# A gated delta-rule block with two WKV stages: a new order for the opening, gates' sums one slot later, and the first inverse in one piece

## The chip, the core and the metric

The kernel runs as one program on one core of a Trainium2 chip. The metric is device time in microseconds (us) of one execution; below, "the profiled execution" is one that was also traced. The engines are TensorE (PE, with its weight loads PEld), VectorE (DVE), ScalarE (ACT), GpSimd (POOL) and SyncE (SP, which issues DMAs).

## The reference

Everything is float32. The inputs are x and a side tensor of 4 batches x 512 tokens x 512 channels, a condition vector per batch, and weights. Cut to what matters:

```python
def wkv(r, k, w, u, cond):                     # v is k here
    tf = sigmoid(sum(cond)); decay = exp(-exp(w)) * (0.5 + 0.5 * tf)
    ek, ekv = exp(min(k, 30)), exp(min(k, 30)) * k
    nf, df = forward scans  a = a * decay + ekv  and  b = b * decay + ek
    nb, db = the same two scans backwards
    euk = exp(min(u + k, 30))
    num, den = nf + nb - ekv + euk * k, df + db - ek + euk
    return sigmoid(r) * num / max(den, 1e-8) * (0.8 + 0.2 * tf)

def attn(c):                                   # c = wkv(x, side, w1, u1, cond)
    q, k, v, z = c @ W_qkvz                    # 16 heads of q, k; 32 heads of v, z; 128 each
    b, a = c @ W_ba
    q, k, v = silu(causal convolution of 4 taps over tokens)
    beta, g = sigmoid(b), -exp(A_log) * softplus(a + dt_bias)
    q, k = rmsnorm(q), rmsnorm(k)              # and constant factors
    for each chunk, with g summed inside it:   # gated delta rule
        T = inverse of (1 + strictly lower part of beta * k k^T * exp(g_i - g_j))
        v_new = T (beta v) - T (beta k exp(g)) state
        out = q exp(g) state + (q k^T * decay) v_new;  state = decayed state + k^T v_new
    return (rmsnorm(out) * norm_w * silu(z)) @ W_out

x = x + attn(wkv(x, side, w1, u1, cond))
x = x + wkv(x, side, w2, u2, cond) @ binarized(ffn_w) + ffn_b
```

## The kernel before

**Units.** The work on the attention is cut into 64 units `n`: batch `b` and head pair `hq` (one head of q and k with its two heads of v and z), `divmod(n, 16)`. A unit works on all 512 tokens of its batch in four chunks of 128. Its weights come in six slabs `r`: q 0, k 1, v 2 and 3, z 4 and 5; in the first batch a slab is loaded raw (`wraw`), turned by PE (`ps_w`), copied by ACT (`w`) and stored for the later batches (`wsc`). Each of q, k and v goes through `project` (`ps_p`, four products), the first `tap` on ACT and three `taps` on DVE (`y`), then `silu`. `square` and `norms` give the norms; the reciprocal square root is a Newton iteration of 12 small operations (`root`, on POOL).

**The key side** of a unit runs six units ahead (`AHEAD`, `K`): `gap_load` brings the running sums of the gates from DRAM (`gsc`) to all partitions (`dkd`, and `dkt` for the query side), `gap_mask` (POOL) and `gap_exp` (ACT, 8 instructions) make decays of them, `key_pairs` (PE, `ps_kk`) and `key_matrix` (DVE, 8 instructions) the matrices, and `key_blocks` stores their 32 x 32 diagonal blocks (`blocks_m`). Four units are a group: their 128 blocks of 32 x 32 come back as one tile `L`, whose triangular inverses are made by 30 steps (`group_step`) of two instructions each. In the loop these run on POOL, for the first group on DVE. `group_end` stores them straight (`blocks_n`) and turned (`Lt`, `blocks_t`), and `inverse_load` brings a unit's own to the places where `inverse_1` to `inverse_4` (PE, with copies between) put the 128 x 128 inverse together: four loads of `inv_t` and six of `inv_n` for a unit, all on SP's queue.

**The gates** of a batch: `gates_product` (`ps_ba`, 32 products), `gates_exp` (ACT), `gates_series` (DVE, some 20 operations on 128 x 128), `gates_sum` (PE, `ps_g`), `gates_keep`, `gates_turn` (`ps_gt`), `gates_rows`, which stores `gsc`. Those of batch b+1 are made in the loop's iteration with `hq == 8`, three times in all.

**The order.** Each engine executes its instructions in the order in which the program writes them: the wrapper `InOrder` (line 80) keeps it, so every instruction of the profile stands under L80 and is told by its tile's name. The loop's iteration `i` walks `plan`, 22 slots of calls, each with an offset: `K` is unit i+6, `F` unit i (query, value, inverse), `C` unit i-1 (the chunks of the recurrence), `O` i-2 (output norm), `W` i-3 (output product). `("sub", m, n)` is a step of the next group, `("gate", f)` one of the gates, `("wkv", f)` a piece of the next batch's WKV, and `jobs` are calls added to a slot of one iteration.

**The opening** stands ahead of the loop. Loads of x and the side tensor go out on ACT's queue, constants on SP's. The first batch's WKV runs in four blocks of 128 channels with tiles lent from later work (`lent_...`): `first_mix` (POOL, a product), `first_scan` (DVE, two scans for "d" and two for "n"), `first_sum` (PE), `first_end` (DVE: limit, reciprocal, product; result `cT`). Its stages are put in an order by a shift of four stages a block, so that `first_mix` of the next block lies beside the scans of the one before. Then come the gates, the key sides of units 0 to 5 together, the first group's steps on DVE, and twenty `inverse_load` DMAs for units 0 and 1. Iteration 0 makes the query, value and z of unit 0, holds the matrices of units 4 and 5 till slot 13, and holds unit 0's inverse till slot 18:

```python
                    elif 0 <= i + rest[0] < NU:
                        if i == 0 and (f in INVERSE or f == gap_load and rest[0] > K):
                            later.append((f, *rest))
                        elif not (i == 0 and f == inverse_load or i == NU + 1 and f == out_start):
                            f(i + rest[0], *rest[1:])
```

PSUM's eight banks belong to tags with turns of their own ("pp" 2, "pj" 3, "inv" 1, "st" 2), and the four raw tiles of `ld` are shared by all slabs.

Of the kernel before, what the change touches and what calls it, by code (L numbers as in the profile page):

```python
# [40 lines left out]
def kernel(  # L41
# [104 lines left out]
    with ExitStack() as main:  # L146
# [24 lines left out]
        for cb in range(KT):  # L171
            at = slice(cb * P, (cb + 1) * P)
            raw = ld.tile([P, NC, P], F32, tag="raw", name=f"raw_k_first_{cb}")
            for t, src in ((raw, fside), (xs[0][:, :, at], x)):
                A.dma_start(out=t, in_=src[0, :, at].rearrange("(c p) d -> p c d", p=P))
            first_raw[cb] = raw

# [4 lines left out]
        for n, v in enumerate((w1, w2, u1, u2)):  # L182
            Q.dma_start(out=wu[:, n, :], in_=v.rearrange("(n p) -> p n", p=P))
        Q.dma_start(out=alog, in_=A_log.partition_broadcast(P))
# [17 lines left out]
        A.activation(nea, alog, AF.Exp)  # L202
        V.tensor_scalar_mul(nea, nea, -1.0)

# [128 lines left out]

        def gates_series(g, part):
# [13 lines left out]
            elif part == 2:  # L348
# [5 lines left out]
                V.tensor_scalar_add(beta[b], beta[b], 1.0)  # L354
                V.reciprocal(beta[b], beta[b])
# [8 lines left out]
        def gates_keep(g):  # L364
# [13 lines left out]
                gsum[b][:, 0].rearrange("p c (q r) -> p q c r", r=2),  # L378
            )

        def gates_turn(g):
            g["pt"] = bank("pj", f"ps_gt_{g['b']}")
            T.transpose(g["pt"][: NC * HV, :P], g["flat"][:, : NC * HV], ident)

        def gates_rows(g):
            b, n = g["b"], NC * HV
            rows = wkp.tile([P, S], F32, tag="d", name=f"sp_r_{b}")
            A.copy(rows[:n, :P], g["pt"][:n, :P])
# [143 lines left out]


# [36 lines left out]
        def key_root(n):  # L570
            root(*units[n]["kroot"])
            key_factors(n)
# [89 lines left out]
        def inverse_load(n):  # L662
# [3 lines left out]
            for d, at in enumerate(blocks):  # L666
# [3 lines left out]
                if d < 3:  # L670
                    for h in range(2):
                        Q.dma_start(
                            out=Tn[blocks[2 * h + (d > 0)], :, at],
                            in_=blocks_n[g, i, d, h * HM : (h + 1) * HM].rearrange("m i j -> i m j"),
                        )
# [363 lines left out]
        def last_add(b, c):  # L1039
# [33 lines left out]
             (slab_start, F, 3), ("gate", gates_series, 2), ("sub", 5, 25)],  # L1073

            [(project, F, 2, 0), (tap, K, 1, 0), (taps, K, 1), (head_end, O, 0),
             ("gate", gates_sum), ("wkv", wkv_mix), ("sub", 6, 26)],

            [(chunk_t, C, 1), (inverse_3, F), ("gate", gates_keep), (chunk_t_end, C, 1), (silu, K, 1),
             ("wkv", wkv_scan, "d", False), (slab_start, F, 0), ("sub", 7, 27)],

            [(project, F, 2, 1), (head_turn, O, 1), (slab_turn, F, 3), ("gate", gates_turn), (inverse_3_end, F), ("wkv", wkv_scan, "d", True),
# [396 lines left out]
```

## Time and profile before

| | |
|---|---|
| median of 3 runs | 3109.1 us (3107.02 to 3109.18) |
| profiled execution | 3108.79 us, its span 3107.0 us, mean granted PE clock 0.983 |
| busy | PE 2988.3 us (96%), DVE 2071.6 (67%), ACT 1866.0 (60%), POOL 1314.7 (42%) |
| instructions | 57961 |
| last block of the first WKV ends (`cT`, DVE) | 63.0 us from the span's start |
| last key matrix of group 0 ends | 114.2 |
| the closing copy `Lt` of the first group ends | 144.2 |
| iteration 1's first product (`ps_w<-vb,inv_t`) | 198.5 |
| iteration 2's first product | 242.4 |

The profile is of one execution. Busy shares are means over the whole span; a stretch of its own is read from the busy times by stretch, what an engine stood idle for from the waits ("engine and tile <- who released it: total, times, longest"), and the path that set the end from the chain of waits (start, duration, what). In all rows the time is in us from the span's start unless the text says otherwise. "Clock" is the share of TensorE's full clock that was granted.

### The profile page before, as it was taken

The numbers are of one execution on the slowest core, as the hardware profiler recorded it, in microseconds if no ns is written. First come the engines' busy times: TensorE is split into PE (matmuls) and PEld (weight loads), VectorE is DVE, ScalarE is ACT, GpSimd is POOL, SyncE is SP. The second block draws the span as 40 slices with busy tenths as digits, with TensorE's granted clock in tenths as the row PEclk, the third lists the DMA queues.
The fourth block names the chain that finished last, engine by engine and source line by source line (L and its number), as shares of the span: only waits on it lengthen the run. The fifth ranks groups of instructions, "written<-read, shape, count | busy, mean of one in ns | idle before, by whom it ended". The sixth has DMA issues, their size and how long they took to land.

```text
span 3107.0 us, 57961 instructions
## 1 busy us (share of the span) xinstructions
PE 2988.3 (96%) x20058; PEld 1978.5 (64%) x20058; DVE 2071.6 (67%) x4738; ACT 1866.0 (60%) x5119; POOL 1314.7 (42%) x3044
## 2 busy tenths in 40 slices
PE   6479999999999999999999999999999999999999
PEld 3346667666666666666666666666666666666665
DVE  7545776667655777777765787777766656577643
ACT  2446766667666666566666666566665666656552
POOL 3215445254432646355442636345451515255313
PEclk9689999999999999999999999999999999999999
DMA  3224544345343432323332332333332342323321
GB/s 75 90 82 139 145 121 131 111 130 156 110 139 101 129 93 82 109 81 114 104 94 76 118 104 82 88 101 115 94 97 68 104 112 79 108 73 115 115 78 61
DMA packets 421875, 320.52 MB, mean 103 GB/s; under 512 B 220176, under 2 KB 329232, under 8 KB 421200
## 3 DMA queue, kind: packets, MB, share of 16 engines
q1 hardware_dynamic: 417360, 314.73, 35.1%
q8 instruction: 160, 2.62, 0.4%
q10 hardware_dynamic: 4224, 2.10, 0.3%
q14 instruction: 131, 1.07, 0.1%
HBM read 246.19 MB, written 70.52 MB: 102 GB/s over the span
## 4 chain that ended last, share of the span: by engine, by line
PE 88%; DVE 6%; ACT 3%; issue 1%; DMA 1%; SPq 0%; POOL 0%; ACTq 0%; DVEq 0%; POOLq 0%
PE ps_p L80 27%; PE ps_z L80 14%; PE ps_out L80 14%; PE ps_s L80 5%; PE ps_w L80 5%; PE ps_o L80 3%; PE ps_st L80 2%; PE ps_j L80 2%; PE ps_kq L80 2%; PE ps_i L80 2%; PE ps_f L80 2%; PE ps_v L80 2%; PE ps_kk L80 2%; PE ps_h L80 1%; PE psn L80 1%
## 5 line engine op out<-in xcount | busy, mean ns | idle before, releaser
L80 PE MATMUL ps_p<-cT,w 128*128 128x512 f32 x2000 | 959.3, 608 | 15.9 <-ACT w L80 15.8
L80 DVE SCALAR_TENSOR_TENSOR y<-ps_p,cw,y 128x511 f32<-128x511 f32 (+2 forms) x768 | 573.1, 746 | 442.8 <-ACT y L80 427.9
L80 PEld LDWEIGHTS ps_p<-cT,w 128*128 128x128 f32 x2000 | 347.4, 192 | 312.3 <-issue 263.9
L80 PE MATMUL ps_z<-w,cT 128*128 128x256 f32 x2048 | 478.2, 380 | 0.0
L80 PE MATMUL ps_out<-wo,hT 128*128 128x512 f32 x1024 | 463.8, 596 | 0.2 <-ACT hT L80 0.2
L80 PEld LDWEIGHTS ps_z<-w,cT 128*128 128x128 f32 x2048 | 374.9, 191 | 43.0
L80 PEld LDWEIGHTS ps_out<-wo,hT 128*128 128x128 f32 x1024 | 184.9, 190 | 186.8 <-issue 179.8
L80 ACT ACT_TABLE_LOAD x141 | 180.9, 1283 | 145.8 <-DVE y L80 121.2
L80 ACT ACTIVATE qs<-ps_s,eg 128x128 f32<-128x128 f32 x384 | 120.4, 364 | 240.2 <-PE ps_j L80 154.7
L80 POOL TENSOR_TENSOR L<-L,t 128x30 f32<-128x30 f32 (+14 forms) x450 | 248.8, 553 | 34.9
L80 POOL TENSOR_SCALAR_AFFINE_SELECT dkd<-dkd 128x1024 f32<-128x1024 f32 x64 | 70.3, 1099 | 456.3 <-DMA dkd<-gsc 325.3
L80 POOL TENSOR_TENSOR t<-L 128x30 f32<-128x30 f32 (+14 forms) x450 | 228.8, 509 | 34.4 <-DMA L<-blocks_m 4.2
L80 ACT ACTIVATE y<-ps_p,cw 128x512 f32<-128x512 f32 x256 | 173.7, 678 | 69.2 <-PE ps_p L80 68.2
L80 POOL TENSOR_TENSOR rs_t_k<-rs_y_k 128x4 f32<-128x4 f32 x174 | 55.8, 321 | 353.7 <-DVE rs_y_k L80 344.6
L80 ACT ACTIVATE junk<-o 128x128 f32<-128x128 f32 x512 | 158.0, 309 | 71.9 <-DVE o L80 63.6
L80 ACT ACTIVATE v<-y 128x512 f32<-128x512 f32 x128 | 80.7, 630 | 198.5 <-DVE y L80 198.4
L80 DVE SCALAR_TENSOR_TENSOR o<-o,rs_y_o,nz 128x128 f32<-128x128 f32 x512 | 188.6, 425 | 1.3 <-POOL rs_y_o L80 1.3
L80 POOL TENSOR_TENSOR rs_t_o<-rs_y_o 128x8 f32<-128x8 f32 x192 | 39.0, 203 | 349.1 <-DVE rs_y_o L80 338.1
L80 DVE SCALAR_TENSOR_TENSOR r<-ps_s,nbe,vb 128x128 f32<-128x128 f32 x384 | 115.8, 343 | 99.7 <-PE ps_s L80 99.7
L80 DVE TENSOR_TENSOR x<-x,ps_out 128x512 f32<-128x512 f32 x256 | 168.8, 679 | 18.3 <-PE ps_out L80 18.1
L80 ACT COPY w<-ps_w 128x256 f32<-128x256 f32 (+1 forms) x346 | 145.3, 430 | 47.5 <-PE ps_w L80 47.2
L80 ACT ACTIVATE dkt<-dkt,gsum 128x128 f32<-128x128 f32 x512 | 162.6, 392 | 12.9 <-POOL dkt L80 12.6
(270 smaller groups left out, 5558.2 us busy)
## 6 DMA issues: line engine op xcount, KB each, us to landing
w<-wsc SPq DMA_DIRECT2D x288, 256.0 KB, 5.1
dkd<-gsc SPq DMA_DIRECT2D x64, 512.0 KB, 4.2
dkt<-gsc SPq DMA_DIRECT2D x64, 512.0 KB, 4.8
wraw<-in_L_attn_W_qkvz_dram SPq DMA_DIRECT2D x96, 256.0 KB, 3.0
wo<-wosc SPq DMA_DIRECT2D x96, 256.0 KB, 3.6
wsc<-w SPq DMA_DIRECT2D x90, 256.0 KB, 2.1
blocks_m<-dkd SPq DMA_DIRECT2D x256, 32.0 KB, 1.7
L<-blocks_m SPq DMA_DIRECT2D x16, 512.0 KB, 5.5
```

Of the source, the lines that this page charges most:

```text
L80: return lambda *args, **kw: tc.keep_in_program_order(op(*args, **kw))
```

## The change

The opening is written anew, and iteration 0 of the loop is part of it; the loop begins at 1. Block 0 of x and side is loaded on ACT's queue, the others on SP's. `first_end` is split into `first_under`, `first_over` (the reciprocal) and `first_end`, and `first_mix` of the next block is called behind `first_over`; slabs are turned in between. Gates' products and the key projections of units 0 and 1 are made block by block. `gates_beta` is split from the series, and `gates_keep` reads PSUM for the rows. The key sides of units 0 to 3 come first, with squares on POOL and roots on DVE (`root_now`); the query, value and z work of unit 0 and parts of units 4 to 6 stand around the first group's steps. Unit 0's `inv_n` loads go to ACT's queue, and its four inverse stages follow one another. What remains of the keys of units 4, 5 and 6 becomes jobs of iteration 1. In the loop's plan `gates_sum` moves from slot 7 to slot 8, behind `chunk_t` and `inverse_3`, and keep, turn and rows to one slot later each. Diff, cut to its core (removed helpers of the old opening are left out):

```diff
+        def first_load(cb, queue):
             at = slice(cb * P, (cb + 1) * P)
             raw = ld.tile([P, NC, P], F32, tag="raw", name=f"raw_k_first_{cb}")
             for t, src in ((raw, fside), (xs[0][:, :, at], x)):
-                A.dma_start(out=t, in_=src[0, :, at].rearrange("(c p) d -> p c d", p=P))
+                queue.dma_start(out=t, in_=src[0, :, at].rearrange("(c p) d -> p c d", p=P))
             first_raw[cb] = raw
+        first_load(0, A)
...
-        for n, v in enumerate((w1, w2, u1, u2)):
+        for n, v in ((0, w1), (1, w2), (2, u1)):
             Q.dma_start(out=wu[:, n, :], in_=v.rearrange("(n p) -> p n", p=P))
+        for cb in range(1, KT):
+            first_load(cb, Q)
+        Q.dma_start(out=wu[:, 3, :], in_=u2.rearrange("(n p) -> p n", p=P))
...
+        def gates_beta(g):
+            b = g["b"]
+            V.tensor_scalar_add(beta[b], beta[b], 1.0)
+            V.reciprocal(beta[b], beta[b])
...
-                V.tensor_scalar_add(beta[b], beta[b], 1.0)
-                V.reciprocal(beta[b], beta[b])
...
-                gsum[b][:, 0].rearrange("p c (q r) -> p q c r", r=2),
+                ps[:, :n].rearrange("p (c q r) -> p q c r", q=HQ, r=2),
...
+        def root_now(v, y, t):
+            for _ in range(3):
+                V.tensor_tensor(t, y, y, ALU.mult)
+                V.scalar_tensor_tensor(t, t, -0.5, v, ALU.mult, ALU.mult)
+                V.scalar_tensor_tensor(y, t, 1.5, y, ALU.add, ALU.mult)
...
-        def inverse_load(n):
+        def inverse_load(n, other=Q):
...
+            for d, at in enumerate(blocks[:3]):
+                for h in range(2):
+                    other.dma_start(
+                        out=Tn[blocks[2 * h + (d > 0)], :, at],
+                        in_=blocks_n[g, i, d, h * HM : (h + 1) * HM].rearrange("m i j -> i m j"),
+                    )
...
-             (slab_start, F, 3), ("gate", gates_series, 2), ("sub", 5, 25)],
+             (slab_start, F, 3), ("gate", gates_series, 2), ("gate", gates_beta), ("sub", 5, 25)],
...
-             ("gate", gates_sum), ("wkv", wkv_mix), ("sub", 6, 26)],
-            [(chunk_t, C, 1), (inverse_3, F), ("gate", gates_keep), (chunk_t_end, C, 1), (silu, K, 1),
+             ("wkv", wkv_mix), ("sub", 6, 26)],
+            [(chunk_t, C, 1), (inverse_3, F), ("gate", gates_sum), (chunk_t_end, C, 1), (silu, K, 1),
...
+            [(project, F, 2, 1), (head_turn, O, 1), (slab_turn, F, 3), ("gate", gates_keep), (inverse_3_end, F), ("wkv", wkv_scan, "d", True),
...
-             ("wkv", wkv_sum, "d"), (slab_start, C, 4), (slab_start, C, 5), ("gate", gates_rows), ("sub", 9, 29)],
-            [(project, F, 3, 0), (norms_turn, K, 1), (slab_turn, F, 0), (inverse_4_end, F), (silu, F, 2),
+            [(project, F, 3, 0), (norms_turn, K, 1), (slab_turn, F, 0), (inverse_4_end, F), (silu, F, 2), ("gate", gates_rows),
...
+        def first_under(w):
+            V.scalar_tensor_tensor(
+                w["df"], w["sum_d"], 1e-8, cT[0][:, w["cb"]], ALU.max, ALU.mult
+            )
+        def first_over(w):
+            V.reciprocal(w["df"], w["df"])
...
+        def first_gates(ks):
+            if ks[0] == 0:
+                g["bank"] = bank("inv", "ps_ba_0")
...
+        def first_key(n, ks):
+            u = unit(n)[-1]
+            if ks[0] == 0:
+                u["pp1"] = bank("pp" if n < 2 else "pj", f"ps_p_{n}_1")
...
+        for n in group0:
+            slab(n, 1, homes[n])
+        slabs.append((wba_start, wba_turn, wba_end))
+        for r in (2, 3, 0):
+            slab(0, r)
+        for n in others:
+            slab(n, 1, homes[n] if n < AHEAD else None)
...
+        first_in(0)
+        first_in(1)
+        first_limit(ws[0])
+        first_mix(ws[0])
         for cb in range(KT):
-            w = wkv_start(0, 0, cb)
...
-        first_key(0)
+            w = ws[cb]
+            first_scan(w, "d")
+            if cb == 0:
+                first_in(2)
+            first_sum(w, "d")
+            slabs_on(2 if cb else 0)
+            first_scan(w, "n")
+            if cb == 0:
+                first_in(3)
+            first_sum(w, "n")
+            if cb:
+                for n in range(2):
+                    first_key(n, (cb - 1,))
+            if cb > 1:
+                first_gates((0, 1) if cb == 2 else (2,))
+            first_under(w)
+            if cb < KT - 1:
+                first_limit(ws[cb + 1])
+            first_over(w)
+            if cb < KT - 1:
+                first_mix(ws[cb + 1])
+                slabs_on(2 if cb else 1)
+            if cb == 0:
+                Q.dma_start(out=cw, in_=conv_w.rearrange("(n p) k -> p n k", p=P))
+            first_end(w)
...
+        first_gates((3,))
+        for n in group0:
+            first_key(n, (3,) if n < 2 else (0, 1, 2, 3))
         gates_exp(g)
-        first_key(1)
+        A.activation(nea, alog, AF.Exp)
+        G.tensor_scalar(nea, nea, -1.0, None, ALU.mult)
+        tap(0, 1, 0)
+        tap(1, 1, 0)
         for part in range(3):
             gates_series(g, part)
         gates_sum(g)
-        first_conv(0)
+        tap(0, 1, 1)
         gates_keep(g)
         gates_turn(g)
         gates_rows(g)
-        for n in range(AHEAD + 1):
+        gap_load(0, "d")
+        gap_load(1, "d")
+        for r in (4, 5):
+            slab_start(0, r)
+        for n in range(2, AHEAD + 1):
             gap_load(n, "d")
         gap_load(0, "t")
-        slab_start(AHEAD, 1)
-        first_key(2, "pj")
-        first_key(3, "pj")
-        first_conv(1)
+        slab_start(AHEAD + 1, 1)
+        tap(0, 1, 2)
+        tap(0, 1, 3)
+        gates_beta(g)
...
+            sq = u["sq1"] = homes[n]
+            G.tensor_tensor(sq, u["x1"], u["x1"], ALU.mult)
...
+        first_silu(0)
+        tap(2, 1, 0)
+        both(project, 0, 2)
+        first_norm(0)
+        key_pairs(0, "st")
+        taps(1, 1)
+        first_silu(1)
+        tap(3, 1, 0)
+        first_norm(1)
+        key_pairs(1, "st")
+        taps(2, 1)
+        for n in (0, 1):
+            gap_mask(n, "d")
+        first_silu(2)
+        tap(0, 2, 0)
+        first_norm(2)
+        key_pairs(2, "inv")
+        first_kn((0, 1))
+        taps(3, 1)
+        first_root((0, 1))
+        first_silu(3)
+        first_norm(3)
+        project(0, 0, 0, "pj")
+        project(0, 0, 1, "pj")
+        key_pairs(3, "pj")
+        both(project, 0, 3)
+        for n in (0, 1):
+            key_factors(n)
+        first_kn((2, 3))
+        for n in (2, 3):
+            gap_mask(n, "d")
         for n in group0:
-            first_silu(n)
-            if n + 2 < GROUP:
-                first_conv(n + 2)
-            first_norm(n, group0, "inv")
-        many = first_root(group0)
-        gap_mask(0, "d")
-        gap_mask(1, "d")
-        root(*many)
+            both(gap_exp, n, "d")
+        for n in (0, 1):
+            first_matrix(n)
+        first_root((2, 3))
+        for n in (2, 3):
+            key_factors(n)
+        gap_mask(0, "t")
         for n in others:
-            first_key(n)
-            first_conv(n)
-        for n in group0:
-            key_factors(n)
-            if n > 1:
-                gap_mask(n, "d")
-            gap_exp(n, "d", 0)
-            gap_exp(n, "d", 1)
-            key_pairs(n, ("st", "st", "inv", "pj")[n])
+            gap_mask(n, "d")
+        for n in (2, 3):
             first_matrix(n)
         group_load(0)
-        for n in others:
-            first_silu(n)
-            first_norm(n, others, "inv")
+        taps(0, 2)
+        tap(0, 3, 0)
+        silu(0, 2)
+        tap(0, 0, 0)
+        taps(0, 3)
+        taps(0, 0)
+        both(gap_exp, 0, "t")
+        project(4, 1, 0, "st")
+        project(4, 1, 1, "st")
+        project(5, 1, 0, "st")
+        project(5, 1, 1, "st")
+        turn(0, 2)
+        turn_end(0, 2)
+        silu(0, 3)
+        silu(0, 0)
+        square(0, 0)
+        for r in (4, 5):
+            slab_turn(0, r)
+            slab_end(0, r)
+        both(z_product, 0, 0)
+        turn(0, 1)
+        turn_end(0, 1)
+        both(z_product, 0, 1)
+        turn(0, 3)
+        turn_end(0, 3)
+        norms(0, 0)
+        norms_copy(0, 0)
+        queries(0)
+        project(6, 1, 0, "pj")
+        project(6, 1, 1, "pj")
+        z_silu(0, 0)
+        z_silu(0, 1)
+        both(gap_exp, 4, "d")
         for j in range(1, BS - 1):
             group_step(0, j, V)
         group_end(0, V.tensor_copy)
-        inverse_load(0)
+        for n in (4, 5):
+            tap(n, 1, 0)
+        inverse_load(0, A)
         inverse_load(1)
-        many = first_root(others)
-        root(*many)
-        for n in others:
-            key_factors(n)
-            gap_mask(n, "d")
-            gap_exp(n, "d", 0)
-            gap_exp(n, "d", 1)
-            key_pairs(n, "st")
+        gap_load(1, "t")
+        both(queries_end, 0)
+        for n in (4, 5):
+            taps(n, 1)
+        for n in (4, 5):
+            silu(n, 1)
+        for n in (4, 5):
+            square(n, 1)
+        inverse_1(0)
+        inverse_1_end(0)
+        inverse_2(0)
+        norms(4, 1)
+        inverse_2_end(0)
+        norms_copy(4, 1)
+        inverse_3(0)
+        norms(5, 1)
+        inverse_3_end(0)
+        norms_copy(5, 1)
+        norms_turn(4, 1)
+        inverse_4(0)
+        inverse_4_end(0)
+        gap_load(AHEAD + 1, "d")
...
-        for i in range(NU - W - 1):
+        for n, slot, tag in ((4, 1, "pj"), (5, 6, "inv"), (6, 12, "inv")):
+            job(1, slot, key_pairs, n, tag)
+        for n, slot in zip(others, (2, 6, 12)):
+            job(1, slot, key_matrix, n, 0)
+            job(1, slot + 1, key_matrix, n, 1)
+            job(1, slot + 1, key_blocks, n)
+        for f in (key_norm, key_root_now):
+            job(1, 0, f, 4)
+        job(1, 2, norms_turn, 5, 1)
+        for f in (key_norm, key_root_now):
+            job(1, 4, f, 5)
+        for half in range(2):
+            job(1, 2, gap_exp, 5, "d", half)
+            job(1, 8, gap_exp, 6, "d", half)
+        job(1, 0, tap, 6, 1, 0)
+        job(1, 1, taps, 6, 1)
+        job(1, 2, silu, 6, 1)
+        job(1, 2, square, 6, 1)
+        job(1, 4, norms, 6, 1)
+        job(1, 4, norms_copy, 6, 1)
+        job(1, 6, norms_turn, 6, 1)
+        for f in (key_norm, key_root_now):
+            job(1, 6, f, 6)
+        def is_made(i, f, n, *args):
+            z = f in (z_product, z_silu) or f in (slab_start, slab_turn, slab_end) and args[0] > 3
+            return z and n == 0 or i == NU + 1 and f == out_start
+        for i in range(1, NU - W - 1):
...
-                        if i == 0 and (f in INVERSE or f == gap_load and rest[0] > K):
-                            later.append((f, *rest))
-                        elif not (i == 0 and f == inverse_load or i == NU + 1 and f == out_start):
-                            f(i + rest[0], *rest[1:])
+                    elif 0 <= i + rest[0] < NU and not is_made(i, f, i + rest[0], *rest[1:]):
+                        f(i + rest[0], *rest[1:])
...
-                if i == 0 and slot == 13:
-                    for n in others:
-                        first_matrix(n)
-                if i == 0 and slot == 18:
-                    for f, *rest in later:
-                        f(rest[0], *rest[1:])
```

## The prediction, made before the change was run

> **What bounds the kernel now.** I read the page first, then busy time by stretches of time, then the waits of PE, the chain of waits, and at last the timelines of DVE, SP and PE around the moved steps. On the page (PE's busy tenths, granted clock) only the first slices of 77.7 us stand out:
>
> ```profile
> PE   6479999999999999999999999999999999999999
> PEclk9689999999999999999999999999999999999999
> ```
>
> From slice 4 on PE is full at full clock, so what is moved there is worth only what PE waits. Slices 1 to 3 are the opening. Busy time by stretch (columns: sum, then PE, PE's weight loads, DVE, ACT, POOL, the clock, DMA share, GB/s); the last two rows are loop iterations 1 and 4:
>
> ```profile
> 110.00:120.00 10.00, 2.75 (x13) 2.67 (x13) 4.20 (x15) 8.42 (x20) 0.00 (x0) 0.54 0.42 86
> 130.00:140.00 10.00, 2.96 (x4) 0.67 (x2) 9.17 (x25) 0.31 (x2) 0.00 (x0) 0.50 0.00 1
> 140.00:150.00 10.00, 0.00 (x0) 0.00 (x0) 4.25 (x16) 0.00 (x0) 3.82 (x20) 0.50 0.33 115
> 150.00:160.00 10.00, 0.17 (x1) 0.17 (x2) 0.00 (x0) 0.00 (x0) 0.00 (x0) 0.50 0.43 89
> 198.49:242.41 43.92, 40.51 (x298) 28.07 (x297) 21.95 (x54) 27.56 (x78) 5.80 (x19) 0.95 0.35 105
> 338.40:386.90 48.50, 47.62 (x337) 32.61 (x336) 35.42 (x77) 32.66 (x88) 17.52 (x34) 1.00 0.40 116
> ```
>
> ACT fills 110 to 120, DVE 120 to 144, then for 12 us nothing computes. The waits of PE up to 242 say on what, and the chain of waits in what order:
>
> ```profile
> PE ps_w L80 <- DMA wraw<-in_L_attn_W_qkvz_dram: 30.4, 2, 26.9
> PE pss_first L80 <- ACT sq L80: 14.3, 5, 10.6
> ```
>
> ```profile
> 111.86 2.35 DVE dkd L80 x8
> ...
> 117.32 3.81 DMA L<-blocks_m
> ...
> 144.24 2.87 DMA blocks_t<-Lt
> ...
> 156.70 3.08 DMA wraw<-in_L_attn_W_qkvz_dram
> ```
>
> The last key matrix of group 0 ends at 114.2; its blocks go out and come back as L (121.15); 60 substitution steps and the closing copies on DVE end at 144.2; the result lands at 147.1; SP issues 20 inverse loads in line from 147.12 (0.46 each); and only behind them the weight slab for which PE has waited 26.9 us (iteration 0's first work, unit 0's values).
>
> **The change part by part.** Sums go against the profiled execution (3108.8; span 3107.0; its median of runs is 0.3 above). Marks are: iteration 1 begins at 198.5, iteration 2 at 242.4.
>
> *First WKV.* DVE carries it from 14 to 63. The timeline of DVE, blocks 1 and 3:
>
> ```profile
> 29.29 2.33 DVE L80 TENSOR_TENSOR_SCAN lent_M<-decay,lent_M 128x512 f32<-128x512 f32 x2
> 31.53 0.74 DVE L80 TENSOR_SCALAR lent_at<-lent_at 128x512 f32<-128x512 f32 x2
> 32.19 4.43 DVE L80 TENSOR_TENSOR_SCAN lent_M<-decay,lent_M 128x512 f32<-128x512 f32 x2
> 37.23 3.35 DVE L80 RECIPROCAL lent_M<-lent_M 128x512 f32<-128x512 f32 x1
> 53.42 1.21 DVE L80 TENSOR_TENSOR_SCAN lent_vb<-decay,lent_vb 128x512 f32<-128x512 f32 x1
> ```
>
> A scan takes 1.2 alone and 2.2 beside POOL's product for the next block. The change puts that product beneath the reciprocal, which took 3.353 in all four blocks, two of them with POOL's product running into it; I take no loss there. A middle block is then 4.69 (four scans, as 53.42 to 58.11 in block 3) + 0.70 + 0.74 + 3.43 + 0.75 = 10.3 for 12.07 now: twice -1.77. At the start ACT issues two loads instead of eight (0.52 each, its first work at 10.69), so I put the first scan at 10.4 for 14.09, the bound being the constants on SP (issue about 2.3, landing as the others after 6.8): block 0 ends at 25.5 for 29.4. The end goes from 63.0 to 55.7: **-7.3** (-2 if POOL and reciprocal do hinder each other).
>
> *Gates.* Now 63.0 to the store of the rows at 77.9, which all decay loads need. Of ps_ba's 32 records (4.13) 8 stay behind the last block (1.03); the reciprocal of beta and three taps (1.17 and 2.2) no longer stand ahead of gsum. Against it PE gets 1.73 and 6.9 of key projections ahead of the sums, ready at 65.4, where DVE alone would be ready at 64.5. Store at 68.6, 12.9 for 14.9 after the WKV: **-2.0** (0 to -4).
>
> *Matrices of group 0.* Now 36.3 from that store to 114.2, since ACT makes the decay exponentials (8 of 0.295 a unit) only after the convolutions of units 4 and 5. The new order makes the same 32 of them (9.4) right after the four silus, about 81 to 90.4. Costs: squares on POOL (1.31 to 2.1 for ACT's 0.63); a root of 11 small DVE operations, by the rows of 0.17 to 0.3 about 2.3 each, the second between matrices 1 and 2. Factors of POOL after it at about 93, two matrices of 2.15, end at 98, 29.4 after the store: **-6.9** (-2 to -10).
>
> *From there to the inverse.* L's way and the substitution stay (30.0): their copies end at 128 for 144.2. Before, 44.5 us followed to inverse_1 at 188.7: 12.5 of loads, 3.1 for the slab, then unit 0's values, query and z from 159.8 to 188. All that now lies in the 22 us of DVE's substitution (PE 0.3 of the window, ACT 0.03) and the 7 us of L's way. Half of the inverse loads go to ACT's queue, ten each at 0.46, so 4.6 for 9.2; landing and first stage at 135, 7 after the copies: **-37.5**. If the cover were too short (PE's work there is some 30 us at half clock against 37), what is left over comes back one for one, 0 to +8. The stages themselves follow without slot 18's other work: 8.5 for 9.75, **-1.2**. Iteration 1 then begins at 143.5, 55 earlier.
>
> *Iteration 1* pays for units 4 to 6. Removed: z and two slabs of unit 0 (PE 6.9 and some 2). Added: three roots (2.3 to 2.9 each), three matrices (2.15 each) and the last taps (2.25) on DVE, about 17; exponentials (2 x 2.36), silu, squares and about three table loads of 1.28 on ACT, about 11; keys' products of some 1 each on PE. By sums no engine is over: PE 36 to 40, DVE 39, ACT 39. But engines keep program order: PE's norms of unit 6 wait for its square on ACT, which waits for the taps on DVE behind two roots and matrix 4; the wraw loads on SP stand behind the storing of matrix blocks 4 and 5, and behind a decay load that waits until inverse_3 has freed its tile; head and state work waits behind them all. No row shows this mix; the bounds are PE alone (38.5) and the two engines DVE and ACT half in series (65). I take 55, nearest to a third of the added 28 us exposed: **+11** for 43.9 (-5 to +21).
>
> *Loop.* From iteration 2 the plan differs only at the three gates. PE's waits there are 2.43, 2.88 and 2.87 (8.2). The sums now come behind chunk_t (0.9) and inverse_3 (0.6): -1.55 each, **-4.6** (0 to -8.2). After the third one the timeline of PE shows more:
>
> ```profile
> 1990.33 0.49 PE L80 MATMUL ps_g<-sp_y,tri_le 128*128 128x128 f32 x2 [2.87 <-DVE sp_y L80]
> ...
> 1993.54 3.78 PE L80 MATMUL ps_p<-cT,w 128*128 128x512 f32 x4
> ```
>
> The same four products take 1.88 at 1985.58: one of three waits halved the clock for a while, worth 1.9 more. The Trainium skill, page "TensorE: Matmul & The Clock Gate", section "Part 1: The HAM clock gate", says that the clock drops only after an idle window of about 3.4 us; this row has it after 2.87, so row and rule differ. By the rule the sum would stand at the 4.6 without any more; by the row it would be 6.5.
> I keep the 1.9 for the lower end only, as two of three waits as long did not do it.
>
> Sum: -7.3 - 2.0 - 6.9 - 37.5 - 1.2 + 11 - 4.6 = -48.5, that is 3108.8 - 48.5 = **3060**.
>
> **The rivals.** *Iteration 1 is PE-paced*: about 44 as now, so 3049. For it: iterations of the loop pack DVE 35 and ACT 33 under PE's 48. Against it: three in-order chains that the loop spreads over three iterations. 0.17.
>
> *The cover gives back*: iteration 1 takes 70 to 75, or a first wait in the cover (z of unit 0 or the slabs behind blocks on SP) holds the inverse by some 15: 3075 to 3088. For it: the waits that go are in-order waits, and the new order is full of them. 0.22.
>
> *The clock makes it slower.* PE's busy time times granted clock, added over stretches of 10 us, is 134 us before iteration 2. If the denser but choppier opening held PE at the half clock seen from 130 to 160 all along, that work would take 268 and iteration 2 begin at 268 for 242.4: +25.6 - 4.6, 3130. It decides from a mean clock of 134/242 = 0.55 downward with PE busy throughout. Against it: the granted clock was 0.9 in slice 0, with PE at 0.6. 0.05.
>
> *It doesn't do what it says*: the substitution's end moves, but the first slab of iteration 1 stands behind the inverse loads as before and the 55 shrink to nothing: 3104 by the gates alone, within 0.2%. 0.03.
>
> **How the numbers follow.** The forecast (3050 to 3072) has 0.53. A difference under 0.2% (6.2 us) is not told from none by this measurement. The range goes from 3042 (iteration 1 at 44, gates 8.2) to 3086 (iteration 1 at 75, contention 5) and leaves out the slower cases and the farthest of both. Faster: the forecast and the first two rivals, 0.92; same 0.02; slower 0.06.
>
> **What would show it.** Right: the row of PE's wait for wraw (26.9) is gone; reciprocals stay 3.35 and all scans 1.2; last row of the opening's cT near 55.7; matrices end near 98, inverse_1 near 135, iteration 1 begins near 143.5 and iteration 2 near 199; ps_g waits 1.3 or less; the steady iterations keep 48.4. Wrong: ps_w or ps_i still waits over 10 us for a DMA; reciprocals of 4 or more; a clock near 0.5 in iteration 1; iteration 2 after 215.

## The result, and the profile after

The changed kernel takes 3075.9 us (median of 4 runs, 3075.2 to 3076.5) against 3108.8 for the kernel before on the same occasion: 0.9895 of it, 95% interval 0.9878 to 0.9912. The profiled execution took 3075.2 us, its span 3073.5. That is 33 us less, not the 48.5 of the sum: inside the range (3042 to 3086), but 4 us above the forecast's own band (3050 to 3072), with a wrong term in it.

The first products of the loop's 64 iterations (`ps_w<-vb,inv_t` on PE's timeline) split the difference without a rest. Their distance to the same mark of the kernel before:

| mark | before | after | difference | step of it |
|---|---|---|---|---|
| iteration 1 begins | 198.49 | 139.32 | -59.2 | -59.2 |
| iteration 2 | 242.41 | 196.51 | -45.9 | +13.3 |
| iteration 3 | 287.98 | 246.74 | -41.2 | +4.7 |
| iteration 9 (first gates done) | 583.93 | 546.02 | -37.9 | +3.3 |
| iteration 25 (second) | 1314.04 | 1281.04 | -33.0 | +4.9 |
| iteration 41 (third) | 2020.94 | 1990.31 | -30.6 | +2.4 |
| iteration 60 | 2845.96 | 2812.39 | -33.6 | -2.9 |

The opening gave more than forecast; iterations 1 and 2 took 18 back, and the three iterations with gates took 10.7 where 4.6 were to be won. On the page, PE's busy tenths and its clock:

```profile
PE   8689999999999999999999999999999999999999
PEclk9789999999999999999999999999999999999999
```

The first three slices are at 8, 6 and 8 (before at 6, 4 and 7). Busy time by stretch (columns as above), the last two rows being iterations 1 and 4:

```profile
110.00:120.00 10.00, 10.00 (x55) 8.12 (x54) 9.21 (x24) 2.85 (x8) 0.00 (x0) 0.92 0.04 11
150.00:160.00 10.00, 5.83 (x21) 3.25 (x22) 2.48 (x11) 6.42 (x20) 0.83 (x4) 0.66 0.13 36
139.32:196.51 57.19, 41.49 (x291) 28.01 (x291) 34.07 (x113) 37.74 (x99) 6.98 (x30) 0.86 0.21 59
295.19:343.64 48.45, 47.57 (x338) 32.61 (x336) 36.18 (x79) 32.56 (x87) 17.70 (x37) 1.00 0.39 119
```

From 110 to 120 DVE makes the substitution and PE is now full beneath it, at clock 0.92. Iteration 4 is as before (48.45). Iteration 1 has no engine that is full: 41.5, 34.1 and 37.7 in 57.2. The waits of PE up to its start, and the chain of waits from the last key matrix to the inverse:

```profile
PE ps_i L80 <- DMA inv_t<-blocks_t: 8.7, 2, 8.3
```

```profile
98.32 3.63 DMA L<-blocks_m
125.09 2.86 DMA blocks_t<-Lt
...
129.37 2.12 DMA inv_t<-blocks_t
131.54 0.68 PE ps_i L80 x30
```

The wait of 26.9 for a slab is gone; what is late next is the inverse's own round trip, 8.3. DVE's timeline of a middle block of the first WKV has scans of 1.2 and the reciprocal unharmed:

```profile
22.62 4.78 DVE L80 TENSOR_TENSOR_SCAN lent_M<-decay,lent_M 128x512 f32<-128x512 f32 x4
28.56 3.35 DVE L80 RECIPROCAL lent_M<-lent_M 128x512 f32<-128x512 f32 x1
```

And PE's timeline in the first iteration with gates (idle time ahead of an instruction and its releaser in brackets):

```profile
511.36 0.49 PE L80 MATMUL ps_g<-sp_y,tri_le 128*128 128x128 f32 x2 [0.95 <-DVE sp_y L80]
...
519.74 1.12 PE L80 MATMUL ps_j<-nw,inv_n 64*64 64x64 f32 x16 [3.20 <-DVE nw L80]
...
521.64 3.43 PE L80 MATMUL ps_p<-cT,w 128*128 128x512 f32 x4
```

The wait for the sums has shrunk to 0.95, as forecast. It was 2.43 before:

```profile
552.60 0.49 PE L80 MATMUL ps_g<-sp_y,tri_le 128*128 128x128 f32 x2 [2.43 <-DVE sp_y L80]
```

But a new wait of 3.20 stands ahead of `ps_j` (inverse_4), and the products behind it run at half clock (3.43 for four, 1.88 at full clock). DVE and ACT show why:

```profile
518.77 0.29 DVE L80 TENSOR_SCALAR gsum<-ps_g 128x128 f32<-128x128 f32 x1 [3.14 <-ACT gsum L80]
518.98 0.28 DVE L80 COPY sp_f<-ps_g 128x128 f32<-128x128 f32 x1
519.18 0.42 DVE L80 COPY nw<-ps_i 128x256 f32<-128x256 f32 x1
```

```profile
514.86 1.28 ACT L80 ACT_TABLE_LOAD   x1 [6.89 <-DVE y L80]
516.15 0.63 ACT L80 ACTIVATE k<-y 128x512 f32<-128x512 f32 x1
516.80 1.28 ACT L80 ACT_TABLE_LOAD   x1
518.10 0.49 ACT L80 ACTIVATE eg<-ps_g 128x384 f32<-128x384 f32 x1
```

`gates_keep`, put one slot later, now stands behind the silu `k<-y` on ACT. That silu waits for DVE's taps until 514.9, and it takes the table that keep's exponential then has to load again. DVE's copy of `gsum` waits for ACT, and the copy `nw`, which PE needs, stands behind it in DVE's order.

### The profile page after: what moved, and what is told of

It is laid out like the page before. It is cut to its first block, busy times and chain, and to the rows that moved or that the text cites. A ratio compares the mean times of both kernels' runs of the same rounds, so it can differ in the third digit from the quotient of the medians.

```text
span 3073.5 us, 58028 instructions
## 1 busy us (share of the span) xinstructions
PE 2986.3 (97%) x20060; PEld 1979.1 (64%) x20060; DVE 2076.0 (68%) x4788; ACT 1878.7 (61%) x5129; POOL 1304.8 (42%) x3013
## 4 chain that ended last, share of the span: by engine, by line
PE 89%; DVE 5%; ACT 3%; issue 1%; DMA 1%; POOL 0%; SPq 0%; DVEq 0%; ACTq 0%; POOLq 0%
PE ps_p L80 27%; PE ps_z L80 14%; PE ps_out L80 14%; PE ps_s L80 5%; PE ps_w L80 5%; PE ps_o L80 3%; PE ps_j L80 3%; PE ps_st L80 2%; PE ps_kq L80 2%; PE ps_f L80 2%; PE ps_i L80 2%; PE ps_v L80 2%; PE ps_kk L80 2%; PE ps_h L80 1%; PE psn L80 1%; DVE y L80 1%
## 5 line engine op out<-in xcount | busy, mean ns | idle before, releaser
L80 ACT ACTIVATE dkt<-dkt,gsum 128x128 f32<-128x128 f32 x512 | 162.5, 392 | 13.7 <-POOL dkt L80 13.5
L80 PEld LDWEIGHTS ps_o<-w,dkt 128*128 128x128 f32 x1024 | 153.7, 192 | 14.6 <-ACT w L80 2.1
```

Of the source, the lines that this page charges most:

```text
L80: return lambda *args, **kw: tc.keep_in_program_order(op(*args, **kw))
```

## The experiments

Where runs have the same opening, their first WKV ended between 52.3 and 54.8 us from one execution to the next. So effects in the opening are counted from an event shortly before them, and those in the loop by the length of an iteration.

**1. The gates put back.** The changed kernel with the old slots in the plan.

```diff
-             ("wkv", wkv_mix), ("sub", 6, 26)],
+             ("gate", gates_sum), ("wkv", wkv_mix), ("sub", 6, 26)],
...
-            [(chunk_t, C, 1), (inverse_3, F), ("gate", gates_sum), (chunk_t_end, C, 1), (silu, K, 1),
+            [(chunk_t, C, 1), (inverse_3, F), ("gate", gates_keep), (chunk_t_end, C, 1), (silu, K, 1),
...
```

The rest of the diff puts turn and rows one slot earlier again.

> The changed kernel with the loop's gates put back to their old slots (sums in slot 7, keep in slot 8 ahead of the silu, turn 9, rows 10). Theory K: the three iterations with gates got longer (58.85, 56.16, 56.80 for 55.51, 51.22, 54.40), because gates_keep now stands behind the silu on ACT, DVE's gsum copy waits for ACT, and the copy nw that inverse_4 needs stands behind gsum. Then the three go back to about 55.5, 51.2 and 54.4, some 10.7 us less, and the whole to about 3065. Rival O: the longer iterations come from the new opening (what it leaves in the queues or pools), then they stay at 58.9, 56.2 and 56.8 and the whole at 3076.

Measured: 55.51, 54.41 and 54.41, 7.5 us less than 58.85, 56.16 and 56.80. The whole is 3070.5 us, 0.9891 of before (0.9875 to 0.9908). Rival O falls. The second is not 51.2 since in this run the wait of 2.87 for the sums halved the clock there (the four products behind took 3.78), as it did in the kernel before only at the third.

**2. Only keep ahead of the silu.**

```diff
-            [(chunk_t, C, 1), (inverse_3, F), ("gate", gates_sum), (chunk_t_end, C, 1), (silu, K, 1),
+            [(chunk_t, C, 1), (inverse_3, F), ("gate", gates_sum), ("gate", gates_keep), (chunk_t_end, C, 1), (silu, K, 1),
...
-            [(project, F, 2, 1), (head_turn, O, 1), (slab_turn, F, 3), ("gate", gates_keep), (inverse_3_end, F), ("wkv", wkv_scan, "d", True),
+            [(project, F, 2, 1), (head_turn, O, 1), (slab_turn, F, 3), (inverse_3_end, F), ("wkv", wkv_scan, "d", True),
```

> The changed kernel with one call moved: gates_keep follows gates_sum in slot 8, ahead of the silu of the key side, the sums stay late. Theory K: PE's wait of 3.2 us for the copy nw and the half clock after it are gone, PE's wait for the sums stays at 0.9 to 1.4, and the gates' iterations are 1.5 us under those of before each: some 54.0, 49.7 and 51, the whole about 3060. Rival L: it is the late sums themselves that cost (everything from the sums to the decay loads comes later); then the iterations stay near 58.9, 56.2 and 56.8 and the whole within 3 us of 3076.

Measured: 3064.2 us, 0.9867 (0.9853 to 0.9882); iterations 55.52, 51.21, 51.21, together 13.9 less than in the changed kernel. Theory K holds and rival L falls. PE's timeline in the first of them:

```profile
513.37 0.49 PE L80 MATMUL ps_g<-sp_y,tri_le 128*128 128x128 f32 x2 [0.95 <-DVE sp_y L80]
...
517.84 0.67 PE L80 MATMUL ps_s<-state,k 128*128 128x256 f32 x2 [0.95 <-DVE state L80]
...
521.28 0.33 PE L80 MATMUL ps_gt<-ident,sp_f 128*128 128x128 f32 x1 [1.35 <-ACT hT L80]
```

The wait for `nw` is gone, and in this run no product behind these waits is at half clock. But the 1.5 us each of the cover did not come: the iterations are 55.5 and 51.2, those that the kernel before has where its clock stays whole. PE's one wait of 2.4 to 2.9 has become several of about 1 that sum to the same. What late sums win is the clock of the second and third iteration with gates. Experiments 6 and 9 to 12 have the same plan, and with this one all twelve of these iterations took 51.2; with the sums early (the kernel before and experiment 1) three of four took 54.4. So the clock is worth 3.2 us there.

In the first iteration with gates the short waits are no safeguard. The three of 0.95, 0.95 and 1.35 stand in all six runs. It took 55.5 in experiments 2, 6 and 10, but 57.2 in 9, 11 and 12, where the products behind the third wait ran at half clock. In experiment 12:

```profile
514.24 0.33 PE L80 MATMUL ps_gt<-ident,sp_f 128*128 128x128 f32 x1 [1.35 <-ACT hT L80]
514.72 3.68 PE L80 MATMUL ps_p<-cT,w 128*128 128x512 f32 x4 [0.16 <-ACT w L80]
```

**3. The gates alone.** The kernel before with the move of sums, keep, turn and rows and nothing else.

> The kernel before with only the move of the gates in the loop (sums to slot 8, keep to 9 behind the silu, turn 10, rows 11). Theory K: the opening as before, the three iterations with gates near 58.9, 56.2 and 56.8, so some 10.7 us more than before, about 3119.5. Rival O (they are long because of the new opening): 55.5, 51.2, 54.4 less the 1.5 each of the cover, about 3104.

Measured: 59.99, 56.73 and 55.38, 11.0 more than before; the whole 3118.4 us, 1.0041 (1.0026 to 1.0056). This part of the change by itself makes the kernel slower. PE's new wait is in it three times, 9.3 us in all.

**4. POOL's product beside the scans again.**

```diff
             w = ws[cb]
+            if cb < KT - 1:
+                first_limit(ws[cb + 1])
+                first_mix(ws[cb + 1])
             first_scan(w, "d")
...
             first_under(w)
-            if cb < KT - 1:
-                first_limit(ws[cb + 1])
             first_over(w)
             if cb < KT - 1:
-                first_mix(ws[cb + 1])
```

> The changed kernel with the next block's limit and POOL product called ahead of the block's scans, beside them as in the kernel before, instead of behind the reciprocal's issue. Theory S (POOL's product slows DVE's scans, the reciprocal not): scans of blocks 0 to 2 go from 1.2 to 2.2 us for some two of four, the last block's end from 52.3 to 56 or 58, and the whole is 4 to 6 us longer, 3080 to 3082. Rival: the first WKV is paced by loads and the turning of slabs on PE, so its end moves by under 1 us.

Measured: the last block ends at 63.9 instead of 52.3, the whole 3088.8 us (one run). The timeline of DVE, block 1:

```profile
27.09 7.68 DVE L80 TENSOR_TENSOR_SCAN lent_M<-decay,lent_M 128x512 f32<-128x512 f32 x4
35.38 3.35 DVE L80 RECIPROCAL lent_M<-lent_M 128x512 f32<-128x512 f32 x1
```

Four scans take 7.68 instead of 4.78, the reciprocal 3.35 in both. Theory S holds and was too small: 3.0 and 3.1 us in blocks 1 and 2, 3.8 in block 0, whose first scan stands behind the second block's limit (14.0 for 9.5), and 1.7 in block 3, where PE's sum comes later.

**5. One queue for unit 0's inverse loads.**

```diff
-        inverse_load(0, A)
+        inverse_load(0)
```

> The changed kernel with unit 0's six inv_n loads on SP's queue too, behind its four inv_t loads, instead of on ACT's. Theory of the prediction (half of the ten loads' issue time stood ahead of the first stage): inverse_1 starts 4.6 us later than 130.8 and iteration 1 as much later than 139.3. Theory Q: inverse_1 needs inv_t alone, which SP issues first in both; only the second stage needs inv_n, so inverse_1 stays at 130.8 and iteration 1 begins 1 to 2.5 us later, at 140.3 to 141.8.

Measured: from the first inverse product to iteration 1 9.7 us instead of 8.5, while that product follows the first load's issue by 2.7 and 2.8. So the second queue is worth 1.2 us, at the second stage: theory Q. (Iteration 1 began at 142.1, but 1.6 of that lies ahead of the loads.) The whole took 3081.6 us in one run.

**6. The exponentials of units 5 and 6 out of iteration 1**, on top of experiment 2.

```diff
             slab_end(0, r)
+        for n in (4, 5):
+            both(gap_exp, n, "d")
         both(z_product, 0, 0)
...
-        both(gap_exp, 4, "d")
+        both(gap_exp, 6, "d")
...
-        for half in range(2):
-            job(1, 2, gap_exp, 5, "d", half)
-            job(1, 8, gap_exp, 6, "d", half)
```

> The run with keep ahead of the silu, and in addition the decay exponentials of units 5 and 6 (16 ACT instructions of 0.3 us, and the table loads around them) taken out of iteration 1: units 4 and 5 are made between the two z products' slabs and the z products of unit 0, beneath the first group's steps on DVE, and unit 6 where unit 4 was. Theory T: iteration 1 (57.2 and 57.6 us) is paced by ACT's queue, where slab copies that PE waits for stand behind exponentials and table loads (ACT busy without a gap from 142 to 156 and from 168 to 176); it shrinks by 4 to 7 us and its start moves by under 1. Rival D: it is paced by DVE (roots, taps, matrices) and by PE's half clock; it shrinks by under 1.5 us.

Measured: iteration 1 takes 53.4 for 57.6 in experiment 2, its start moved by -0.7; 3061.1 us, 0.9860 (0.9844 to 0.9876). Theory T holds in size, at the low end of its range: ACT's queue paces a part of iteration 1. But it named the wrong wait of PE: the one for the slab copy stays (3.13 in experiment 2, 3.36 here), and the one for ACT's square ahead of a norm falls from 4.07 to 0.52.

**7. The cover taken away.** All of unit 0's query, value and z work and the key projections of units 4 to 6 behind the inverse loads.

```diff
-        taps(0, 2)
-        tap(0, 3, 0)
...
-        both(gap_exp, 4, "d")
         for j in range(1, BS - 1):
             group_step(0, j, V)
         group_end(0, V.tensor_copy)
...
         inverse_load(1)
+        taps(0, 2)
+        tap(0, 3, 0)
...
+        both(gap_exp, 4, "d")
```

> The changed kernel with unit 0's query, value and z work and the key projections of units 4 to 6 (all that stood between the load of L and the first group's steps) called behind the inverse loads instead, as the kernel before had most of it behind them. Theory C (the 37.5 us of the prediction come from doing this work beneath the substitution): the steps on DVE begin up to 7 us earlier, but inverse_1 stands behind the moved work on PE, and iteration 1 begins 20 to 30 us later than 139.3. Rival: what counted was only the loads' queue and the slab behind it; then iteration 1 begins at most 10 us later.

Measured: iteration 1 begins at 171.8, 32.5 later, and every iteration up to 57 is as in the changed kernel; 3109.2 us, the time of the kernel before. Theory C holds, a little above its range. The waits of PE from 95 to 200 begin with

```profile
PE ps_v L80 <- ACT v L80: 32.7, 1, 32.7
```

It is the idle stretch of the kernel before in another place.

**8. Squares of group 0 on ACT.**

```diff
-            G.tensor_tensor(sq, u["x1"], u["x1"], ALU.mult)
+            A.activation(sq, u["x1"], AF.Square)
```

> The changed kernel with the squares of units 0 to 3 on ACT (0.63 us each) instead of POOL (1.04 us). Theory P: POOL makes the square of unit 2 only behind two masks, PE's norm waits 3.3 us for it and DVE's taps of unit 3 stand 4.4 us behind the norm; with ACT the last matrix of the group ends about 2 us before 95.2, and iteration 1 begins 2 us before 139.3. Rival A: ACT gets as much longer as POOL got shorter and the exponentials come later by 2.5; the matrices end at 95 to 97.

Measured: the last matrix ends at 94.9 for 95.2, and iteration 1 begins at 138.8; the whole 3072.5 (one run). Theory P falls, and the delay of rival A is not there either: DVE's wait for the norms stays at 4.3. PE has eight products `ps_p` (5.37 us, from 66.9) ahead of the norms; that these pace them is a reading of the timeline, which experiment 9 tests.

**9. Those products behind the norms**, on top of experiment 6.

```diff
-        both(project, 0, 2)
         first_norm(0)
...
-        tap(0, 2, 0)
         first_norm(2)
         key_pairs(2, "inv")
+        both(project, 0, 2)
...
+        tap(0, 2, 0)
```

> The run with the exponentials early, and in addition unit 0's first value projection (8 products, 5.4 us at half clock) called behind the norms and pairs of units 0 to 2 instead of ahead of the first norm, its tap behind group 0's exponentials. Theory N (with the squares on ACT nothing moved, since PE's 5.4 us stand ahead of the three norms, and DVE waits 4.3 us for the third before the taps of unit 3): DVE's wait goes to about 1, silu 3 and the exponentials start 3 us earlier, the last matrix ends at 92 to 93 and iteration 1 begins 2 to 3 us earlier. Rival X: the end is set by the landing of the decay loads and the masks; then the matrices end within 0.7 us of where they did.

Measured: the wrong way. DVE's wait went from 4.4 to 6.4, iteration 1 began 2.8 later, the whole 3064.5 (one run). PE's timeline has the reason:

```profile
70.85 1.87 PE L80 MATMUL ps_g<-ones,lent_nz 128*128 128x1 f32 x8 [4.17 <-POOL lent_nz L80]
72.58 2.05 PE L80 MATMUL ps_kk<-k 128*128 128x128 f32 x8
```

Without the products PE stood idle for 4.17 us; the norms began 1.9 earlier (70.85 for 72.74 in experiment 6), but they and the pairs then ran at half clock, 1.87 and 2.05 for 0.95 and 1.14. The work that stood in the way also kept the clock up.

**10. Two roots of iteration 1 on POOL**, on top of experiment 6.

```diff
-        for f in (key_norm, key_root_now):
+        for f in (key_norm, key_root):
             job(1, 4, f, 5)
...
-        for f in (key_norm, key_root_now):
+        for f in (key_norm, key_root):
             job(1, 6, f, 6)
```

> The run with the exponentials early, and in addition the roots of units 5 and 6 in iteration 1 on POOL (12 operations of 0.28 us each, some 3.4 us, as for all later units) instead of DVE (2.2 us each). Theory D2 (what is left of iteration 1's length is DVE's order: inverse_3's bank is freed only by the matrix of unit 5, which stands behind the root and the taps of unit 6; PE waits 4.1 us there): the wait falls to about 2 and iteration 1 goes from 53.4 to 50.5 to 52. Rival: the wait stays, since the matrix waits for POOL's factors instead; 53 to 55.

Measured: iteration 1 takes 50.5 for 53.4, PE's wait ahead of inverse_3 2.3 for 4.1; 3053.5 us in one run, the lowest time seen. Theory D2. Not all of that time is the edit's: of the 7.2 us under the profiled execution of experiment 6, 2.9 stand in iteration 1, 1.3 ahead of it and 2.9 in iterations 58 and 59, which the edit does not touch.

**11. Experiments 9 and 10 together.**

> The last two edits together. If they work on different stages, their gains add: some 4 to 6 us under the 3061 of the run with the exponentials early, 3055 to 3057; if one takes the other's place, 3058 to 3061.

Measured: 3061.8 us, 0.9861 (0.9842 to 0.9881). Iteration 1 has 50.8, as in experiment 10, and begins at 143.5, as late as in experiment 9: one edit gives, the other takes.

**12. Experiment 10 with unit 6's silu later.**

```diff
-        job(1, 2, silu, 6, 1)
-        job(1, 2, square, 6, 1)
-        job(1, 4, norms, 6, 1)
-        job(1, 4, norms_copy, 6, 1)
+        job(1, 4, silu, 6, 1)
+        job(1, 4, square, 6, 1)
+        job(1, 5, norms, 6, 1)
+        job(1, 5, norms_copy, 6, 1)
```

> The run with two roots on POOL, and in addition unit 6's silu and square in iteration 1 moved from slot 2 to slot 4 (behind the exponentials of unit 1's query side) and its norms from slot 4 to 5, so that ACT loads its tables twice less ahead of the slab copy for which PE waits 3.4 us and of the next silu. Theory T (ACT's queue ahead of that copy still paces iteration 1): the copy comes 3 us earlier, PE's wait for it is under 1 us, iteration 1 goes from 50.5 to 47 to 49, the whole to some 3051. Rival: the wait passes to the norms of unit 6, which now come later on ACT; iteration 1 stays within 1 us of 50.5, the whole at 3053.

Measured: 3058.3 us (median of 4), 0.9853 (0.9837 to 0.9870). Iteration 1 has 50.8: the wait for the slab copy fell from 3.4 to 0.4, and that for the norm's square came up to 2.5. The rival is right. It has the lowest median of the versions with more than one run; its interval overlaps those of experiments 2, 6 and 11.

## Why the prediction was right and where it was wrong

By its own steps, from the marks of the two profiles:

| step | forecast | measured |
|---|---|---|
| first WKV (63.0 to 52.3) | -7.3 | -10.7 |
| gates to the store (14.9 to 13.3) | -2.0 | -1.6 |
| matrices of group 0 (36.3 to 29.6) | -6.9 | -6.7 |
| L, substitution, copies (30.0 to 29.8) | 0 | -0.2 |
| from there to inverse_1 (44.5 to 5.8) | -37.5 | -38.7 |
| stages of the inverse (9.75 to 8.5) | -1.2 | -1.3 |
| iteration 1 | +11 | +13.3 |
| iteration 2 | 0 | +4.7 |
| three gates | -4.6 | +10.7 |
| iterations 58 and 59 | 0 | -2.9 |
| sum | -48.5 | -33.4 |

**Right.** The main term, the cover, was right in size and in reason: without it the whole gain is gone (experiment 7). The WKV term had the right mechanism (experiment 4). That POOL's product leaves the reciprocal alone rested on little: before, it ran into three of them (the prediction says two) by under 0.5 us each. Now it lies beneath three of them (POOL from 28.45 to 32.34 in block 1), and they still take 3.35. The term was too small because block 0 ended at 22.7, not 25.5: its first scan starts at 9.5, and only 1.1 us is lost between its scans. Inside the main term the loads' share was wrong: the prediction split the twenty loads ten and ten, 4.6 us for 9.2. In fact six go to ACT's queue and fourteen stay on SP's, and one queue or two, the first stage follows the first load's issue by 2.7 to 2.8; the second queue is worth 1.2, at the second stage (experiment 5). The total held all the same: from the copies to the first stage it counted 7 us, and 5.8 were measured.

**Luck.** The gates missed by 15.3 us and iterations 1 and 2 by 7.0. The first WKV (3.4), the way to inverse_1 (1.2) and iterations 58 and 59 (2.9) gave 7.5 of it back. The last of these is chance. Iteration 58 took 39.8 to 39.9 us in the changed kernel and experiments 1, 8 and 10, and 41.5 to 42.5 in the eight other runs with the new opening, where no edit bears on it; before it took 41.5. Iteration 59 took 47.8 before and again in experiment 4, 46.4 in the changed kernel. The time lies where the second rival put it (3075 to 3088), but neither of that rival's reasons came true: iteration 1 took 57.2, not 70 to 75, and inverse_1 came at 130.9, earlier than the 135 forecast. And the range's lower end, 3042, is 2 us lower than its terms make it (3060 - 11 - 3.6 - 1.9).

**Wrong: the loop's gates.** The step said "The sums now come behind chunk_t (0.9) and inverse_3 (0.6): -1.55 each". It priced the call that was moved against PE's wait alone. Four calls were moved, and keep went past a silu on ACT and ahead of inverse_3_end on DVE. Both were to be read off the plan: ACT's instruction behind the silu waits for the taps, DVE's copy behind that, PE's stage behind both. Experiment 3 has this step alone, experiment 2 takes it out by one call. Even the -1.55 was not there: with keep in its place the wait only spreads. The term should have been 0 without the clock, and with it up to -3.2 in the second and third iteration with gates and up to +1.7 in the first (experiments 9, 11 and 12). The half clock itself was priced too low: 1.9, by four products alone, where the second and third of these iterations in the kernel before, 51.22 and 54.40, have it at 3.2.

**Mis-sized: iterations 1 and 2.** For iteration 1 the 11 was near, and two of the named chains are shown as parts of it: ACT's exponentials and table loads 4.2 us (experiment 6), DVE's roots 2.9 (experiment 10). The rest, 50.5 against 43.9, is not taken apart further. That iteration 2 pays as well was not forecast; "from iteration 2 the plan differs only at the three gates" left out that what iteration 1 leaves behind can differ too. Its first long products (`ps_p`) begin 11.6 us after its start, where they began 8.2 us after it in the kernel before. They wait for a slab copy on ACT, and ACT waits for POOL. ACT's and PE's timelines before:

```profile
245.30 2.45 ACT L80 ACTIVATE dkd<-dkd,gsum 128x128 f32<-128x128 f32 x8
250.58 3.63 PE L80 MATMUL ps_p<-cT,w 128*128 128x512 f32 x4 [3.13 <-ACT w L80]
```

And after:

```profile
203.28 2.45 ACT L80 ACTIVATE dkd<-dkd,gsum 128x128 f32<-128x128 f32 x8 [3.49 <-POOL dkd L80]
208.15 3.78 PE L80 MATMUL ps_p<-cT,w 128*128 128x512 f32 x4 [3.71 <-ACT w L80]
```

After, POOL masks the decays (`dkd`, 202.0) behind the root of the output norm (from 198.6); before, it did so ahead of it (242.0 and 243.6). That makes 3.5 of the 4.7 us, by the traces; no run varied POOL's order. PE's clock is not the reason for them: it is 0.63 instead of 0.87 in these first 13.5 us, but the products begin 11.6 to 11.7 us into the iteration in all twelve runs with the new opening, those too whose small products there ran at full speed (experiments 8 and 12). Why POOL's order differs is open. The plan names the root first in both kernels, while in iteration 3 the mask comes first in both (288.0 and 289.2 before, 246.6 and 247.8 after), so on POOL the order of the plan isn't always the order of execution. The other 1.2 us lie behind these products, at a clock of 0.95 for 1.00; the whole iteration takes 48.8 to 50.4 us in the twelve runs.

**The clock.** The rule in the Trainium skill (page "TensorE: Matmul & The Clock Gate", section "Part 1: The HAM clock gate") asks for an idle window of about 3.4 us, and says that the window runs freely. In these runs waits of 3.15 to 3.20 halved the clock in all three gates of the changed kernel; 2.87 and 2.88 did so in one of two gates of the kernel before and in both of experiment 1; 3.75, in iteration 59 of the changed kernel, did not. Waits of 0.95, 0.95 and 1.35 within 9 us did so in three of six runs. So lengths under the rule's are enough at times, and a length above it not always: that one wait has either outcome agrees with a free window, the length does not. By the rule only the waits would count in the three gates, which are 1.2, 2.7 and 2.7 longer; against iterations at full clock (55.51, 51.2 and 51.2) they take 3.3, 4.9 and 5.6 more, so 2.1 to 2.9 of each is half clock.

## What to carry to other kernels

When a call moves in a hand-written order, write down for each of its instructions, on each engine, what it now stands behind and what now stands behind it; the sum of the one wait that the move is meant to shorten is not its price. Idle time beneath a long serial chain on one engine is where work should be moved first: it carried this whole change. And where PE waits, count the half clock after the wait too: filler work ahead of a wait can be worth more than its own length. Splitting a wait helps, but is no guarantee: two waits of 1.4 us kept the clock in twelve of twelve iterations, where one of 2.9 lost it in three of four, and three of about 1 us lost it in three of six.

## What the runs showed of the hardware

- Work that keeps PE busy can shorten what follows: 5.4 us of products taken away ahead of eight small ones made these twice as long (0.95 to 1.87) and the path 2.8 us longer (experiment 9).
- The same wait of PE may or may not halve the clock: 2.88 and 2.87 in two iterations of one execution, without and with it; the price was 3.2 us (51.22 and 54.40).
- Short waits add up: 0.95, 0.95 and 1.35 us within 9 us halved the clock in three of six runs (four products 3.24 to 3.68 for 1.98; the iteration 57.2 for 55.5).
- Beside POOL's products of two tensors, four DVE scans take 7.68 for 4.78; a reciprocal of the same tile stays at 3.35.
